# One of the seven block products of a hidden layer done by seven products of its own blocks

## The chip, the cores and the metric

One core of a Trainium2 chip. The metric is the device time of one launch in microseconds (us), the median of three runs. All numbers are fp32 unless said otherwise.

## What is computed

4096 tokens of 512 features pass a modulated linear layer; each of 8 experts then picks the 1024 tokens with its highest softmax score, runs a two-layer network on them and adds the result, times the score, to the tokens' rows. Most of the work is in the two `einsum`s over the experts.

```python
y = clip(einsum('blc,oc->blo', x * styles, weight) * dcoefs + bias, -256, 256)
scores = softmax(y @ Wr)                        # 4096 x 8
G, idx = top_k(scores.T, 1024)                  # for each expert
h = gelu(einsum('ekd,edh->ekh', y[idx], W1) + b1)     # 512 -> 2048
X_e = einsum('ekh,ehd->ekd', h, W2) + b2              # 2048 -> 512
out = x + zeros.at[idx].add(G * X_e)
```

## The kernel before

**The frame.** A first part (about the first 180 us) makes the layer's output y, its scores and the first expert's token list. Then follow 16 passes: `for e in range(E)` over 8 experts and `for p in range(NP)` over two halves of the hidden width (L1205 to L1228). A pass has a hidden stage (W1 times tokens, 1024 hidden values of 1024 tokens, into the tile H) and an output stage (H times W2, added into the rows of `out` by an indirect DMA on GpSimd, L1156).

**Seven products for eight.** Both stages cut their matrices in two by two blocks and use the scheme with seven block products and fifteen sums. The functions are named after the products: p1 and p2 make the first block of the result; p6, p7, p5, p3, p4 the others. p1, p6, p5 and p3 all add into one PSUM bank, "a": p1 starts it, ScalarE copies the bank out (`snap`, L1059 for hidden, L1123 for output), p6 adds to it, and so on, so that each later product of "a" must wait for the copy of the state before. p7 and p4 share a bank "c" in the same way, p2 has a bank "b". The sums of one operand are made by `left_sums` (L929 to L932: s3, s1, s2, s4), those of the weights by `weight_sum_steps` (L190 to L193: t1, t2, t4, t3), all on VectorE.

**A hidden unit** (`hidden_unit`, L1031) is one of four row blocks of 128 hidden values; each of its seven products is two matmuls (contraction 256) of 512 tokens. p2 is the product of block "12" of the tokens with block (1,0) of W1; its bank is added to p1's copy (L1072) and passed through Gelu (L1073). p5's copy minus bank "c" (L1087) and bank "c" plus p6's copy (L1096) give two other blocks, p3's bank the last; each goes through Gelu into H.

**An output unit** (`out_unit`, L1102) is one of four blocks of 128 tokens (and of 128 more in the other half); its products are four matmuls each (contraction 512) of 256 columns. Its operand's sums are made from H into tiles hs_o. p1 needs the block of H that p1 and p2 of the hidden units make, p2 that of p3, and p6 needs s2, to which every block but one of H contributes; the last to come is that of p4.

**What sets the order.** `in_turns` (L999) calls the steps: p1 of a unit, then the p3 that the unit before still owes, p2, then the p4 owed, then p6, p7, p5. Work "between" (the sums of weights, the next expert's indices and gathers `fetch`, its token preparation `prepare`, and `route_others` in the first pass, which finds the other experts' thresholds by counting) is tied behind a unit by `issue_after`. Otherwise a scheduler chooses the order on each engine: `product` (L1025) issues its matmuls without `in_order`, so that matmuls of one stage can be placed among those of another. `in_order` (L77) ties each instruction behind the one before on TensorE.

**Feeding.** Weights come by DMA on the SP queue: `load_w1` of the next pass is called after the hidden stage, `load_w2` after the output stage. The next expert's tokens are gathered row by row on GpSimd (L913) into four buffers with the tag "row", written to DRAM from there by the SP queue (L917), read back in another layout (L919) and transposed on VectorE (L952). The token lists come from `indices` (L834): VectorE compares places with a row of numbers (L849, one instruction of 4096 elements), TensorE sums (L855), VectorE rounds (L860).

Of the kernel before, what the change touches and what calls it, by code (L numbers as in the profile page):

```python
# [20 lines left out]
P = 128  # L21
# [4 lines left out]
def tile_modulated_expert_choice_ffn(  # L26
# [73 lines left out]


    NL = P // E
    pk = const.tile([P, P], I32, name="pk")
    nc.gpsimd.iota(pk, pattern=[[0, P]], base=0, channel_multiplier=1)
    pm = const.tile([P, P], I32, name="pm")
    nc.gpsimd.iota(pm, pattern=[[1, P]], base=0, channel_multiplier=0)
    ek = const.tile([P, P], I32, name="ek")
    nc.vector.tensor_scalar(ek, pk, E - 1, None, op0=ALU.bitwise_and)
    em = const.tile([P, P], I32, name="em")
    nc.vector.tensor_scalar(em, pm, E - 1, None, op0=ALU.bitwise_and)  # L110
    same = const.tile([P, P], BF16, name="same")
    nc.vector.tensor_tensor(same, ek, em, ALU.is_equal)
    ahead = const.tile([P, P], BF16, name="ahead")
    nc.vector.tensor_tensor(ahead, pk, pm, ALU.is_lt)
    nc.vector.tensor_mul(ahead, ahead, same)


    iota_lo = const.tile([P, P], BF16, name="iota_lo")
# [44 lines left out]
    HP = HC // NP  # L163
    U = HP // 2
    QD = D // 2
    w1_blocks, w2_blocks = {}, {}

    def weight_blocks(kind, where, name):
# [26 lines left out]
    def weight_sums(kind, blk, name):  # L195
        for _ in weight_sum_steps(kind, blk, name):
            pass

    def load_w1(e, ps):
        where = {}  # L200
# [535 lines left out]

    def route_others():

        ST = rt.tile([P, 2, P], F32, tag="ST", name="ST")
# [12 lines left out]

        mark = rt.tile([P, 2, P], F32, tag="run", name="mark")
# [17 lines left out]

        def ranks(mask, name):

            run = rt.tile([P, 2, P], F32, tag="run", name=f"run_{name}")
# [12 lines left out]
            nc.vector.tensor_copy(off, ps)  # L789
            return run, off  # L790


        sel = rt.tile([P, 2, P], F32, name="sel")
# [3 lines left out]
        eq = rt.tile([P, 2, P], F32, name="eq")  # L797
# [19 lines left out]
        for h in range(2):  # L817
            nc.tensor.transpose(ps[:, h, :], pos[:, h, :], ident)

        pos_i = rt.tile([P, NT, E], I32, tag="ST", name="pos_i")  # L820
        nc.vector.tensor_scalar(pos_i.rearrange("p t e -> p (t e)"),
                                ps.rearrange("p h m -> p (h m)"), -1.0, None, op0=ALU.add)
        part = rt.tile([P, NT, E], I32, tag="part", name="part")
# [3 lines left out]
        part2 = rt.tile([P, NT, E], I32, tag="part", name="part2")  # L827
        nc.vector.tensor_scalar(part2, pos_i, 7, None, op0=ALU.logical_shift_right)
        hi = rt.tile([P, NT, E], BF16, name="hi")
        nc.vector.tensor_copy(hi, part2)  # L830
        for e in range(1, E):
            places[e] = lo[:, :, e], hi[:, :, e]

    def indices(e):  # L834

        lo, hi = places[e]
        oh = gp.tile([P, 2 * GH * YW], BF16, tag="xg", name=f"oh_{e}")[:, 0 : NT * P].rearrange(
            "p (t m) -> p t m", m=P)
        hot = rt2.tile([P, NT, KG], BF16, tag="hot", name=f"hot_{e}")
        nc.vector.tensor_tensor(  # L840
            hot, hi.unsqueeze(2).to_broadcast([P, NT, KG]),
            iota_hi[:, 0:KG].unsqueeze(1).to_broadcast([P, NT, KG]), ALU.is_equal,
        )
        val = rt2.tile([P, NT, 2, KG], BF16, tag="val", name=f"val_{e}")
        nc.vector.tensor_scalar_mul(val[:, :, 0, :], hot, iota_p[:, 0:1])
        nc.vector.tensor_tensor(
            val[:, :, 1, :], hot, iota_t.unsqueeze(2).to_broadcast([P, NT, KG]), ALU.mult
        )
        nc.vector.tensor_tensor(  # L849
            oh, lo.unsqueeze(2).to_broadcast([P, NT, P]),  # L850
            iota_lo.unsqueeze(1).to_broadcast([P, NT, P]), ALU.is_equal,
        )
        ps = ps_small.tile([P, 2, KG], F32, tag="small", name=f"ps_idx{e}")
        for t in range(NT):
            nc.tensor.matmul(ps.rearrange("p a k -> p (a k)"), oh[:, t, :],  # L855
                             val[:, t, :, :].rearrange("p a k -> p (a k)"),
                             start=(t == 0), stop=(t == NT - 1))
# [46 lines left out]
    def gather(e, i):  # L904
# [31 lines left out]
    def token_tiles(e):  # L936
# [6 lines left out]
        tokens[e] = {**s, "11": xT[0, 0], "12": xT[0, 1], "22": xT[1, 1]}, gain, ngain  # L943
        return xT, s, gain, ngain

    def prepare(e):

        xT, s, gain, ngain = token_tiles(e)
# [5 lines left out]
                    xg[:, :, 2 * k * TB : 2 * (k + 1) * TB].rearrange("p t (j a) -> p t j a", a=TB))  # L954
        nc.vector.tensor_scalar_mul(ngain, gain, -1.0)
        left_sums(xT[0, 0], xT[0, 1], xT[1, 0], xT[1, 1], s)

    def first_tokens(started):

# [39 lines left out]
    def in_turns(units, between):  # L999

# [4 lines left out]
        for n in range(len(units)):  # L1005
# [15 lines left out]
            held = unit[5:]  # L1021
        for f in held:
            f()

    def product(ps, lefts, rights, start):  # L1025
        n = len(lefts)
        for k in range(n):
            nc.tensor.matmul(ps, lefts[k], rights[k], start=(start and k == 0), stop=(k == n - 1),  # L1028
                             skip_group_check=True)

    def hidden_unit(e, p, u, H, early=False):  # L1031

# [7 lines left out]
        def mm(ps, left, right, start):  # L1040
            s = tokens[e][0]
            product(ps, [blk[right][:, k, u * P : (u + 1) * P] for k in range(2)],
                    [s[left][:, k, :] for k in range(2)], start)

        def begin(cols):
            s = tokens[e][0]

# [7 lines left out]
                                     skip_group_check=True))  # L1055

        def snap(n):
            t = sp.tile([P, HALF], F32, tag=f"snap{n}", name=f"snap{n}_{name}")
            nc.scalar.copy(t, st["a"])  # L1059
            return t  # L1060

# [3 lines left out]
                mm(st["a"], "11", (0, 0), True)  # L1065
            st["s1"] = snap(1)

        def p2():
            if not early:
                st["b"] = bank("b", name, 1)  # L1070
                mm(st["b"], "12", (1, 0), True)
            added = nc.vector.tensor_add(st["b"], st["b"], st["s1"])  # L1072
            nc.scalar.activation(out[0, 0], st["b"], AF.Gelu, bias=bias[0])  # L1073
            return added

        def p6():
# [20 lines left out]
            nc.scalar.activation(out[1, 0], st["c"], AF.Gelu, bias=bias[0])  # L1097

        unit = [p1, p2, p6, p7, p5, p3, p4]
        return (begin, unit) if early else unit  # L1100

    def out_unit(e, p, v, H, b2_sb):  # L1102

# [101 lines left out]
    for e in range(E):  # L1205
        b2_sb = fx.tile([P, D], F32, tag="b2", name=f"b2_{e}")
        nc.sync.dma_start(b2_sb, b2[e, :].partition_broadcast(P))
        for p in range(NP):
# [60 lines left out]
```

## Time and profile before

| what | value |
|---|---|
| runs | 1745.69, 1746.89, 1747.21 us; median 1746.89 |
| profiled execution | 1745.7 us; its span, first to last instruction, 1743.9 us; granted clock 0.996 |
| VectorE, ScalarE, GpSimd busy | 830.8, 480.2, 293.5 us |
| fp32 matmul of a hidden unit, 512 columns | 593 ns recorded each, two records a matmul |
| fp32 matmul of an output unit, 256 columns | 380 ns recorded each, two records a matmul |
| weight load of 128 columns | 190 ns |
| copy of a bank by ScalarE, 512 and 256 columns | 582 and 474 ns |
| add of a bank on VectorE, 512 and 256 columns | 699 and about 480 ns |
| sum of 512, 1024 elements in SBUF on VectorE | 687, about 1217 ns |
| comparison with the row of numbers, L849 | 4418 ns, seven times |
| gather of 128 rows, issue to landing | 4.3 us |

How to read the profile: matmuls are pipelined, so a recorded duration is longer than the distance from one to the next; the chain that ended last counts each only for the time in which nothing later had started, which is the price in a stream. "PEld" is TensorE's weight load, which overlaps with matmuls. In a line of the timeline, the bracket at the end holds how long the engine stood idle before the instruction and what it waited for. Names are those of the program, with "_h" for hidden and "_o" for output.

### The profile page before, as it was taken

How to read it: one execution, taken by the hardware profiler on the slowest of the kernel's cores; microseconds unless marked ns; L12 is line 12 of the kernel's file. 1: busy time of each engine (PE TensorE's matmuls, PEld its weight loads, DVE VectorE, ACT ScalarE, POOL GpSimd, SP SyncE). 2: the span in 40 equal slices, each digit the busy share in tenths (PEclk: the TensorE clock that was granted, in tenths of full speed). 3: DMA queues.
4: the chain of work that ended last, by engine and by line, in shares of the span. 5: the costliest groups of instructions: out<-in, count | busy, mean ns of one | idle time of the engine just before them, and what ended most of it. 6: DMA issues, size and time to landing. Idle time of an engine off the chain costs nothing.

```text
span 1743.9 us, 17415 instructions
## 1 busy us (share of the span) xinstructions
PE 1718.0 (99%) x6646; PEld 1136.2 (65%) x6646; DVE 830.8 (48%) x1467; ACT 480.2 (28%) x845; POOL 293.5 (17%) x238
## 2 busy tenths in 40 slices
PE   9998999999999999999999999999999999999997
PEld 5775475665748485766758485766758484756656
DVE  5885884524535254624535254614444254614341
ACT  3543312223131322222231313222231313222231
POOL 0112013020212013110312012110302012110202
PEclk9999999999999999999999999999999999999999
DMA  9625527441574237442574237432564137332403
GB/s 207 171 50 197 192 55 179 106 85 49 97 201 73 48 61 183 90 85 55 100 191 85 49 63 176 90 79 55 112 179 90 46 64 186 75 79 61 85 0 49
DMA packets 143252, 178.59 MB, mean 102 GB/s; under 512 B 16825, under 2 KB 92857, under 8 KB 143041
## 3 DMA queue, kind: packets, MB, share of 16 engines
q1 hardware_dynamic: 118240, 115.19, 24.4%
q0 software_dynamic: 24912, 62.27, 21.0%
q8 instruction: 52, 0.85, 0.2%
q14 instruction: 32, 0.25, 0.0%
q10 hardware_dynamic: 16, 0.02, 0.0%
HBM read 120.46 MB, written 65.37 MB: 107 GB/s over the span
## 4 chain that ended last, share of the span: by engine, by line
PE 93%; DVE 4%; ACT 1%; issue 1%; DMA 1%; POOL 0%; POOLq 0%; DVEq 0%; ACTq 0%
PE ps_a_o L1028 25%; PE ps_a_h L1028 23%; PE ps_c_o L1028 12%; PE ps_c_h L1028 12%; PE ps_b_o L1028 6%; PE ps_b_h L1028 6%; PE ps_ya L81 2%; PE ps_yc L81 1%; DVE oh L849 1%; PE ps_y L81 1%; ACT xmT L500 1%; DVE mark L760 1%; PE ps_yt L727 1%; PE ps_a_h_a L1028 0%; PE ps_yb L81 0%
## 5 line engine op out<-in xcount | busy, mean ns | idle before, releaser
L1156 POOL DMA_INDIRECT out<-o_o,idx x128 | 213.2, 1666 | 1246.7 <-DVE o_o L1153 497.0
L1028 PE MATMUL ps_a_o<-w_t,hs_o 128*128 128x256 f32 x1024 | 243.3, 380 | 1.2
L1028 PE MATMUL ps_a_h<-xs,w_t 128*128 128x512 f32 x496 | 233.4, 592 | 0.0
L1028 PEld LDWEIGHTS ps_a_o<-w_t,hs_o 128*128 128x128 f32 x1024 | 192.3, 190 | 33.7 <-issue 7.2
L1028 PEld LDWEIGHTS ps_a_h<-xs,w_t 128*128 128x128 f32 x496 | 94.1, 190 | 119.1 <-issue 118.5
L1059 ACT COPY snap_h<-ps_a_h 128x512 f32<-128x512 f32 x186 | 108.2, 582 | 230.0 <-PE ps_a_h L1028 227.0
L1123 ACT ACTIVATE snap_o<-ps_a_o,gain 128x256 f32<-128x256 f32 x128 | 60.6, 474 | 346.7 <-PE ps_a_o L1028 346.7
L1087 DVE TENSOR_TENSOR snap_h<-snap_h,ps_c_h 128x512 f32<-128x512 f32 x64 | 43.9, 687 | 217.5 <-ACT snap_h L1059 217.5
L1072 DVE TENSOR_TENSOR ps_b_h<-ps_b_h,snap_h 128x512 f32<-128x512 f32 x62 | 43.4, 699 | 202.6 <-PE ps_b_h L1028 202.6
L1028 PE MATMUL ps_c_o<-w,hs_o 128*128 128x256 f32 x512 | 124.2, 380 | 0.0
L1028 PE MATMUL ps_a_o<-w,H 128*128 128x256 f32 x512 | 124.0, 379 | 0.0
L1028 PE MATMUL ps_a_o<-w,hs_o 128*128 128x256 f32 x512 | 121.6, 380 | 0.0
L1028 PE MATMUL ps_b_o<-w,H 128*128 128x256 f32 x512 | 121.1, 379 | 0.0
L1028 PE MATMUL ps_a_h<-xT,w 128*128 128x512 f32 x248 | 120.7, 594 | 0.0
L1028 PE MATMUL ps_c_h<-xs,w 128*128 128x512 f32 x256 | 120.5, 593 | 0.0
L1028 PE MATMUL ps_c_h<-xT,w_t 128*128 128x512 f32 x256 | 120.5, 593 | 0.0
L1028 PE MATMUL ps_c_o<-w_t,H 128*128 128x256 f32 x504 | 119.1, 379 | 0.0
L1028 PE MATMUL ps_a_h<-xs,w 128*128 128x512 f32 x248 | 118.2, 599 | 0.0
L1028 PE MATMUL ps_b_h<-xT,w 128*128 128x512 f32 x248 | 116.8, 593 | 0.0
L1028 PEld LDWEIGHTS ps_a_o<-w,H 128*128 128x128 f32 x512 | 97.1, 190 | 27.0 <-issue 15.5
L1028 PEld LDWEIGHTS ps_a_o<-w,hs_o 128*128 128x128 f32 x512 | 95.9, 190 | 21.8 <-ACT snap_o L1123 9.2
L1028 PEld LDWEIGHTS ps_c_o<-w,hs_o 128*128 128x128 f32 x512 | 97.0, 190 | 13.9 <-issue 0.6
(277 smaller groups left out, 1983.8 us busy)
## 6 DMA issues: line engine op xcount, KB each, us to landing
w<-in_w SPq DMA_DIRECT2D x120, 512.0 KB, 4.1
rows<-row SPq DMA_DIRECT2D x56, 260.0 KB, 3.9
xg<-rows SPq DMA_DIRECT2D x56, 256.0 KB, 6.4
x<-in_x SPq DMA_DIRECT2D x28, 256.0 KB, 8.4
y_dram<-ytok SPq DMA_DIRECT2D x5, 1024.0 KB, 4.3
w<-in_w SPq DMA_DIRECT2D x32, 128.0 KB, 3.5
y_dram<-ytok POOLq DMA_DIRECT2D x12, 256.0 KB, 5.0
b<-in_b SPq DMA_DIRECT2D x8, 256.0 KB, 4.2
```

The source lines that it names most:

```text
L81: behind[engine] = make()
L500: nc.scalar.mul(t, t, styles[1][:, j, b : b + 1])
L727: nc.tensor.transpose(ps[:, o * P : (o + 1) * P], yT[:, o, t * P : (t + 1) * P], ident)
L760: nc.vector.tensor_scalar(mark, ST, cand[:, c + 1 : c + 2].bitcast(F32), None, op0=ALU.is_ge, op1=ALU.add, accum_out=cnt[:, c : c + 1])
L849: nc.vector.tensor_tensor(oh, lo.unsqueeze(2).to_broadcast([P, NT, P]), iota_lo.unsqueeze(1).to_broadcast([P, NT, P]), ALU.is_equal,)
L1028: nc.tensor.matmul(ps, lefts[k], rights[k], start=(start and k == 0), stop=(k == n - 1), skip_group_check=True)
L1059: nc.scalar.copy(t, st["a"])
L1072: added = nc.vector.tensor_add(st["b"], st["b"], st["s1"])
L1087: nc.vector.tensor_add(st["u4"], st["u4"], st["c"])
L1123: nc.scalar.mul(t, st["a"], scale)
L1156: nc.gpsimd.indirect_dma_start(out=last_rows[g] if e == E - 1 else out_rows, out_offset=bass.IndirectOffsetOnAxis(ap=idx[:, e, g : g + 1], ...
```

## The change

In every hidden stage but the first, p2 is no longer two matmuls a unit. Its operands (W1's block (1,0): 256 by 512; the tokens' block "12": 256 by 512) are cut in two by two once more, and the same seven-product scheme runs on blocks of 128 by 256 and 128 by 256, for two row blocks r of 128 (and of 128 more). That makes 14 products of one matmul each, 256 columns wide, in place of 8 matmuls of 512 columns. Each has a bank of its own from the pools "t" (a and c) or "b"; results are collected in a tile q, and p2 of a unit becomes an addition of a part of q to p1's copy, in SBUF.

`hidden_stage` writes the order by hand: the 14 products stand one by one behind products of the units, which now run in the order 0, 2, 1, 3. `product` issues every matmul through `in_order`, in both stages. The p3 and p4 that the last output unit owes are held over into the next hidden stage and run behind its first p1 and p6; `load_w2` is called behind that p4.

The sums for the second level are added: four of 256 elements per weight block (in `weight_sums`) and four per token block (`second_sums`). To find room in SBUF, several buffers are shared or dropped: "row" has three buffers, not four; s1 of an output unit is written over its part of H (the block (1,0)) instead of into a tile of its own; the tiles of `route_others` lie in the row buffers; the second sums lie in the buffer of a token block no longer needed. `indices` does its comparison in four instructions of 1024 elements.

```diff
@@ weight_sums
+        if kind == "w1":
+            b = {(k, j): blk[1, 0][:, k, j * Q : (j + 1) * Q] for k in range(2) for j in range(2)}
+            t = wpool.tile([P, 3, Q], F32, tag="w1_l2", name=f"w1_l2_{name}")
+            t1, t2, t4 = [t[:, n, :] for n in range(3)]
+            nc.vector.tensor_add(t1, b[0, 0], b[0, 1])
+            nc.vector.tensor_add(t2, t1, b[1, 1])
+            nc.vector.tensor_add(t4, t2, b[1, 0])
+            nc.vector.tensor_add(b[0, 1], b[0, 1], b[1, 1])
+            blk["l2"] = {**b, "t1": t1, "t2": t2, "t3": b[0, 1], "t4": t4}
@@ indices
-        nc.vector.tensor_tensor(
-            oh, lo.unsqueeze(2).to_broadcast([P, NT, P]),
-            iota_lo.unsqueeze(1).to_broadcast([P, NT, P]), ALU.is_equal,
-        )
+        for n in range(4):
+            here = slice(n * NT // 4, (n + 1) * NT // 4)
+            nc.vector.tensor_tensor(
+                oh[:, here, :], lo[:, here].unsqueeze(2).to_broadcast([P, NT // 4, P]),
+                iota_lo.unsqueeze(1).to_broadcast([P, NT // 4, P]), ALU.is_equal,
+            )
@@ gather
-            to = gp.tile([P, YW], F32, tag="row", name=f"row_{e}_{g}", bufs=4)
+            to = gp.tile([P, YW], F32, tag="row", name=f"row_{e}_{g}", bufs=3)
@@ new
+    def second_sums(e):
+        s = tokens[e][0]
+        a = {(i, k): s["12"][:, k, i * Q : (i + 1) * Q] for i in range(2) for k in range(2)}
+        t = fx.tile([P, 4, Q], F32, tag="xT10", name=f"x2_{e}")
+        s2 = {f"s{n + 1}": t[:, n, :] for n in range(4)}
+        left_sums(a[0, 0], a[0, 1], a[1, 0], a[1, 1], s2)
+        tokens[e][0]["l2"] = {**s2, "11": a[0, 0], "12": a[0, 1], "22": a[1, 1]}
@@ product
-            nc.tensor.matmul(ps, lefts[k], rights[k], start=(start and k == 0), stop=(k == n - 1),
-                             skip_group_check=True)
+            in_order(partial(nc.tensor.matmul, ps, lefts[k], rights[k], start=(start and k == 0),
+                             stop=(k == n - 1), skip_group_check=True))
@@ new
+    def second_level(e, p, r):
...
+        def mm(tag, left, right, start):
+            if start:
+                st[tag] = (bank("b", f"q{name}", 1) if tag == "b" else
+                           ps_t.tile([P, HALF], F32, tag="t", name=f"ps_q{tag}_{name}"))[:, 0:Q]
+            product(st[tag], [blk[right][:, r * P : (r + 1) * P]], [s[left]], start)
...
+        def p5():
+            mm("a", "s1", "t1", False)
+            st["u4"] = snap(4, -1.0)
+            nc.vector.tensor_sub(out[1, 1], st["u4"], st["c"])
...
+    def hidden_stage(e, p, H, between, held, then):
+        unit = {u: hidden_unit(e, p, u, H) for u in range(U)}
+        steps, results = zip(*[second_level(e, p, r) for r in range(2)])
...
+        plan = [
+            (0, [partial(second, 0)], [partial(second, 0)], [partial(second, 0)], [partial(second, 0)],
+             [partial(second, 0)], []),
+            (2, [], [partial(second, 0)], [partial(second, 0), partial(finish, 0), partial(finish, 2)],
+             [partial(second, 1)], [partial(second, 1)], [partial(second, 1)]),
+            (1, [partial(second, 1)], [partial(second, 1)], [], [partial(second, 1)],
+             [partial(second, 1), partial(finish, 1)], []),
+            (3, [partial(finish, 3)], [], [], [], [], []),
+        ]
+        for n, (u, *fill) in enumerate(plan):
+            p1, _, p6, p7, p5, p3, p4 = unit[u]
+            for f, behind_it in zip((p1, held[0], p6, held[1], p7, p5), fill):
+                f()
+                if n == 0 and f is held[1]:
+                    then()
+                for step in behind_it:
+                    mark = step() or mark
...
+            held = [p3, p4]
+        for f in held:
+            f()
@@ hidden_unit
-        def p2():
-            if not early:
-                st["b"] = bank("b", name, 1)
-                mm(st["b"], "12", (1, 0), True)
-            added = nc.vector.tensor_add(st["b"], st["b"], st["s1"])
-            nc.scalar.activation(out[0, 0], st["b"], AF.Gelu, bias=bias[0])
+        def p2(other=None):
+            to = st["s1"] if other is not None else st["b"]
+            added = nc.vector.tensor_add(to, st["b"] if other is None else other, st["s1"])
+            nc.scalar.activation(out[0, 0], to, AF.Gelu, bias=bias[0])
             return added
@@ out_unit
-             for n in ("s1", "s2", "s3", "s4")}
+             for n in ("s2", "s3", "s4")}
+        s["s1"] = a[1, 0]
         left_sums(a[0, 0], a[0, 1], a[1, 0], a[1, 1], s)
@@ main loop
-            units = [partial(hidden_unit, e, p, u, H) for u in range(U)]
             if e == p == 0:
+                units = [partial(hidden_unit, e, p, u, H) for u in range(U)]
                 units[0:2] = [lambda unit=unit: unit for _, unit in early]
-            in_turns(units, work)
+                in_turns(units, work)
+            else:
+                hidden_stage(e, p, H, work, held, partial(load_w2, e, p))
...
-            in_turns([partial(out_unit, e, p, v, H, b2_sb) for v in range(GH)], work)
-            if nxt[0] < E:
-                load_w2(*nxt)
+            if e == p == 0:
+                work[0] = [partial(second_sums, 0)]
+            held = in_turns([partial(out_unit, e, p, v, H, b2_sb) for v in range(GH)], work,
+                            keep=nxt[0] < E)
```

More of the change, by code (lines that the diff above doesn't have):

```diff
@@ L102, in tile_modulated_expert_choice_ffn @@
     NL = P // E
[L103 to L110, printed above, removed]
     same = const.tile([P, P], BF16, name="same")
-    nc.vector.tensor_tensor(same, ek, em, ALU.is_equal)
     ahead = const.tile([P, P], BF16, name="ahead")
-    nc.vector.tensor_tensor(ahead, pk, pm, ALU.is_lt)
-    nc.vector.tensor_mul(ahead, ahead, same)
+    with tc.tile_pool(name="init", bufs=1) as init:
+        pk = init.tile([P, P], I32, name="pk")
+        nc.gpsimd.iota(pk, pattern=[[0, P]], base=0, channel_multiplier=1)
+        pm = init.tile([P, P], I32, name="pm")
+        nc.gpsimd.iota(pm, pattern=[[1, P]], base=0, channel_multiplier=0)
+        ek = init.tile([P, P], I32, name="ek")
+        nc.vector.tensor_scalar(ek, pk, E - 1, None, op0=ALU.bitwise_and)
+        em = init.tile([P, P], I32, name="em")
+        nc.vector.tensor_scalar(em, pm, E - 1, None, op0=ALU.bitwise_and)
+        nc.vector.tensor_tensor(same, ek, em, ALU.is_equal)
+        nc.vector.tensor_tensor(ahead, pk, pm, ALU.is_lt)
+        nc.vector.tensor_mul(ahead, ahead, same)
     iota_lo = const.tile([P, P], BF16, name="iota_lo")
@@ L165, in tile_modulated_expert_choice_ffn @@
     QD = D // 2
+    Q = HALF // 2
     w1_blocks, w2_blocks = {}, {}
@@ L737, in route_others @@
     def route_others():
-        ST = rt.tile([P, 2, P], F32, tag="ST", name="ST")
+        spare = [gp.tile([P, YW], F32, tag="row", name=f"spare{n}", bufs=3) for n in range(3)]
+        ST, run_, sel, eq, part_ = [
+            spare[n // 2][:, n % 2 * 2 * P : (n % 2 + 1) * 2 * P].rearrange("p (h t) -> p h t", t=P)
+            for n in range(5)]
         ps = ps_t.tile([P, 2, P], F32, tag="t", name="ps_ST")
@@ L751, in total @@
             return ps
-        mark = rt.tile([P, 2, P], F32, tag="run", name="mark")
+        mark = run_
         cand = two_bits[:, 0, :]
@@ L774, in ranks @@
         def ranks(mask, name):
-            run = rt.tile([P, 2, P], F32, tag="run", name=f"run_{name}")
+            run = run_
             nc.vector.tensor_tensor_scan(run.rearrange("p h t -> p (h t)"),
@@ L790, in ranks @@
             return run, off
-        sel = rt.tile([P, 2, P], F32, name="sel")
         cnt = rt2.tile([P, 1], BF16, tag="cnt", name="cnt_gt")
@@ L796, in route_others @@
         tot = total(cnt, "gt")
-        eq = rt.tile([P, 2, P], F32, name="eq")
         nc.vector.tensor_scalar(eq, ST, thr, None, op0=ALU.is_equal)
@@ L818, in route_others @@
             nc.tensor.transpose(ps[:, h, :], pos[:, h, :], ident)
-        pos_i = rt.tile([P, NT, E], I32, tag="ST", name="pos_i")
+        pos_i, part = [t.bitcast(I32).rearrange("p h t -> p (h t)").rearrange("p (t e) -> p t e", e=E)
+                       for t in (ST, part_)]
         nc.vector.tensor_scalar(pos_i.rearrange("p t e -> p (t e)"),
                                 ps.rearrange("p h m -> p (h m)"), -1.0, None, op0=ALU.add)
-        part = rt.tile([P, NT, E], I32, tag="part", name="part")
         nc.vector.tensor_scalar(part, pos_i, P - 1, None, op0=ALU.bitwise_and)
@@ L826, in route_others @@
         nc.vector.tensor_copy(lo, part)
-        part2 = rt.tile([P, NT, E], I32, tag="part", name="part2")
-        nc.vector.tensor_scalar(part2, pos_i, 7, None, op0=ALU.logical_shift_right)
+        nc.vector.tensor_scalar(part, pos_i, 7, None, op0=ALU.logical_shift_right)
         hi = rt.tile([P, NT, E], BF16, name="hi")
-        nc.vector.tensor_copy(hi, part2)
+        nc.vector.tensor_copy(hi, part)
         for e in range(1, E):
@@ L956, in prepare @@
         left_sums(xT[0, 0], xT[0, 1], xT[1, 0], xT[1, 1], s)
+        second_sums(e)
     def first_tokens(started):
@@ L997, in bank, with in_turns @@
         return ps_mm.tile([P, HALF], F32, tag=tag, name=f"ps_{tag}_{name}", bufs=bufs)
-    def in_turns(units, between):
+    def in_turns(units, between, keep=False):
         held = []
@@ L1021, in in_turns @@
             held = unit[5:]
+        if keep:
+            return held
         for f in held:
@@ L1027, in product, with snap, p1, p2 @@
         for k in range(n):
-            nc.tensor.matmul(ps, lefts[k], rights[k], start=(start and k == 0), stop=(k == n - 1),
-                             skip_group_check=True)
+            in_order(partial(nc.tensor.matmul, ps, lefts[k], rights[k], start=(start and k == 0),
+                             stop=(k == n - 1), skip_group_check=True))
+    def second_level(e, p, r):
+        s, blk = tokens[e][0]["l2"], w1_blocks[e, p]["l2"]
+        name = f"{e}_{p}_{r}"
+        q = sp.tile([P, 2, HALF], F32, tag="q", name=f"q_{name}", bufs=1)
+        out = {(i, j): q[:, j, i * Q : (i + 1) * Q] for i in range(2) for j in range(2)}
+        st = {}
+        def mm(tag, left, right, start):
[3 more added lines that the diff above has]
+            product(st[tag], [blk[right][:, r * P : (r + 1) * P]], [s[left]], start)
+        def snap(n, scale=1.0):
+            t = sp.tile([P, Q], F32, tag=f"q{n}", name=f"q{n}_{name}", bufs=1)
+            nc.scalar.mul(t, st["a"], scale)
+            return t
+        def p1():
+            mm("a", "11", (0, 0), True)
+            st["s1"] = snap(1)
+        def p2():
+            mm("b", "12", (1, 0), True)
+            return nc.vector.tensor_add(out[0, 0], st["b"], st["s1"])
+        def p6():
+            mm("a", "s2", "t2", False)
+            st["u2"] = snap(2)
+        def p7():
+            mm("c", "s3", "t3", True)
+        def p5():
+            mm("a", "s1", "t1", False)
+            st["u4"] = snap(4, -1.0)
+            nc.vector.tensor_sub(out[1, 1], st["u4"], st["c"])
+        def p3():
+            mm("a", "s4", (1, 1), False)
+            nc.scalar.mul(out[0, 1], st["a"], -1.0)
+        def p4():
+            mm("c", "22", "t4", False)
+            nc.vector.tensor_add(out[1, 0], st["c"], st["u2"])
+        return [p1, p2, p6, p7, p5, p3, p4], q
@@ new lines, in hidden_stage, with finish, second @@
+    def hidden_stage(e, p, H, between, held, then):
+        unit = {u: hidden_unit(e, p, u, H) for u in range(U)}
+        steps, results = zip(*[second_level(e, p, r) for r in range(2)])
+        g = [iter(x) for x in steps]
+        def finish(u):
+            return unit[u][1](results[u % 2][:, u // 2, :])
+        def second(r, n=1):
+            for _ in range(n):
+                done = next(g[r])()
+            return done
+        mark = None
+        plan = [
[15 more added lines that the diff above has]
+                    mark = step() or mark
+            for work in between.get(n, ()):
+                with tc.issue_after(mark.ins):
+                    work()
+            held = [p3, p4]
+        for f in held:
+            f()
@@ L1043, in mm, with second_product @@
                     [s[left][:, k, :] for k in range(2)], start)
+        def second_product():
+            st["b"] = bank("b", name, 1)
+            mm(st["b"], "12", (1, 0), True)
+            return p2()
         def begin(cols):
@@ L1057, in snap @@
         def snap(n):
-            t = sp.tile([P, HALF], F32, tag=f"snap{n}", name=f"snap{n}_{name}")
+            t = sp.tile([P, HALF], F32, tag=f"snap{n}", name=f"snap{n}_{name}",
+                        bufs=3 if n == 1 else 2)
             nc.scalar.copy(t, st["a"])
@@ L1099, in hidden_unit @@
         unit = [p1, p2, p6, p7, p5, p3, p4]
-        return (begin, unit) if early else unit
+        if early:
+            return begin, unit
+        if e == p == 0:
+            unit[1] = second_product
+        return unit
     def out_unit(e, p, v, H, b2_sb):
@@ L1225, in tile_modulated_expert_choice_ffn @@
                 work[0] = [partial(prepare, e + 1)]
-            in_turns([partial(out_unit, e, p, v, H, b2_sb) for v in range(GH)], work)
-            if nxt[0] < E:
-                load_w2(*nxt)
+            if e == p == 0:
+                work[0] = [partial(second_sums, 0)]
+            held = in_turns([partial(out_unit, e, p, v, H, b2_sb) for v in range(GH)], work,
+                            keep=nxt[0] < E)
 def kernel(**inputs):
```

## The prediction

> **What bounds the kernel now.** I read the page first, for the busy shares and the chain that ended last; columns are busy time, share and instruction count, then shares of the span.
>
> ```profile
> PE 1718.0 (99%) x6646; PEld 1136.2 (65%) x6646; DVE 830.8 (48%) x1467; ACT 480.2 (28%) x845; POOL 293.5 (17%) x238
> PE 93%; DVE 4%; ACT 1%; issue 1%; DMA 1%; POOL 0%; POOLq 0%; DVEq 0%; ACTq 0%
> ```
>
> The chain is TensorE for 93% of the span, so time is won or lost only in TensorE's own queue: in the matmuls that stand there, and in the moments when it waits between two. The second view is busy time by stretches, cut at the same point of four successive passes (one pass is a hidden stage and an output stage; columns: length, PE busy, PEld busy, DVE, ACT, POOL, clock, DMA share, GB/s).
>
> ```profile
> 421.46:519.47 98.01, 97.88 (x369) 64.25 (x369) 44.39 (x62) 25.42 (x45) 21.61 (x16) 1.00 0.58 132
> 519.47:616.38 96.91, 96.83 (x338) 63.55 (x337) 41.85 (x57) 25.32 (x45) 12.96 (x8) 1.00 0.31 66
> ```
>
> A pass takes 96.9 us, or 98.0 where the next expert's indices are computed (32 small matmuls, 0.96 us, and their surroundings). VectorE works 42 to 44 us of it, ScalarE 25: both have room. The third view is the chain across the seam between a hidden and an output stage (start, length, work; _h is hidden, _o output).
>
> ```profile
> 414.45 1.72 PE ps_a_h L1028 x4
> 416.16 0.86 PE ps_a_o L1028 x4
> 417.03 1.85 PE ps_a_h L1028 x4
> 418.88 1.72 PE ps_c_h L1028 x4
> 420.60 0.86 PE ps_a_o L1028 x4
> 421.46 1.73 PE ps_b_o L1028 x8
> 423.19 0.86 PE ps_c_o L1028 x4
> 424.05 0.08 issue
> 424.13 1.96 PE ps_a_o L1028 x8
> 426.09 0.86 PE ps_c_o L1028 x4
> ```
>
> Two things are to be seen. The price of a matmul instruction: 1.72/4 = 0.429 us at 512 columns, 1.73/8 = 0.216 at 256 (each fp32 matmul is two instructions). And the scheduler has filled the seam: half of the output's p1 (0.86) lies between the last unit's p5 and p3, and half of its p7 (0.86) ahead of its p6. The check: 4 x 7 x 4 x 0.429 = 48.1 us and 4 x 7 x 8 x 0.216 = 48.4 make 96.4 of the 96.9, so 0.5 us is lost per pass, 0.44 of it here: 1.85 for 1.72, 0.08, and 1.96 for 1.73. The fourth view is the timeline of the same seam, the other engines' instructions that these waits hang on.
>
> ```profile
> 416.26 0.59 ACT L1059 COPY snap_h<-ps_a_h 128x512 f32<-128x512 f32 x1 [2.85 <-PE ps_a_h L1028]
> 416.89 0.30 PEld L1028 LDWEIGHTS ps_a_h<-xs,w 128*128 128x128 f32 x2 [0.27 <-ACT snap_h L1059]
> 420.63 0.70 DVE L1096 TENSOR_TENSOR ps_c_h<-ps_c_h,snap_h 128x512 f32<-128x512 f32 x1 [3.07 <-PE ps_c_h L1028]
> 421.37 0.69 ACT L1097 ACTIVATE H<-ps_c_h,b_sb 128x512 f32<-128x512 f32 x1 [1.76 <-DVE ps_c_h L1096]
> 422.09 0.69 DVE L929 TENSOR_TENSOR hs_o<-H 128x512 f32<-128x512 f32 x1 [0.75 <-ACT H L1097]
> 422.69 0.69 DVE L930 TENSOR_TENSOR hs_o<-H 128x512 f32<-128x512 f32 x1
> 423.30 0.69 DVE L931 SCALAR_TENSOR_TENSOR hs_o<-hs_o,H 128x512 f32<-128x512 f32 x1
> 423.90 0.68 DVE L929 TENSOR_TENSOR hs_o<-H 128x512 f32<-128x512 f32 x1
> ```
>
> p3 may not load its weights before the copy of p5's bank is done (416.89); the output's p6 waits for p4, its add, its Gelu and the sums s3, s1, s2 (423.99).
>
> **What the Trainium skill says.** "TensorE: Matmul & The Clock Gate", Back-to-back issue gap: in a stream of weight loads and matmuls the spacing is set by both. That would threaten narrow products; here the load takes 190 ns under a spacing of 216, so 256 columns still stream, as the output stage shows. "VectorE: DVE Perf Modes", The DRAIN you can't avoid: the next operation waits until the pipe is empty, and a semaphore between two costs nothing extra. The trace agrees: dependent and independent sums both follow at 0.60 to 0.61. So a sum put ahead of another delays it by 0.60.
>
> **The change, part by part.** *The product replaced.* In 15 of 16 hidden stages (not the first) p2 was 4 units x 4 instructions x 0.429 = 6.87 us of TensorE. In its place: 2 row blocks x 7 products x 2 instructions of 256 columns = 28 x 0.216 = 6.05. Saved: 0.82 us a stage, on the path. Instructions at this width and size fill the output stage, so the price is shown.
>
> *Its waits.* Each bank that is copied and then added to needs about 0.7 us (0.10 + 0.59) of other matmuls between. In the written order the shortest cover is one 512-wide product (1.72) everywhere, or 2.6 in the first unit (0.43 + 1.73 + 0.43), but for one place: the last unit's p5 and p3, which follow each other.
>
> *The seam.* All products now go out in written order, and the changed program's instruction order confirms that nothing of the output stage stands between p5, p3 and p4 or ahead of p6. p3's release is the same copy, so p3 still ends 2.72 us after p5 (416.16 to 418.88) and p4 after 4.44; but the 0.86 of p1 that was done inside this time is now done later. Then come p1 and p2, 3.46 us, and p6, which waits for s2. VectorE's order here is no longer s3, s1, s2: s1 is written over part of H and s3 of the second output unit stands ahead of it in all 15 stages, so s2 is 0.60 later. Before, p6 ended 426.09 - 420.60 = 5.49 after p4; now 6.09. From p5 to the end of p6: 4.44 + 6.09 = 10.53, against 9.93 before, which held 0.86 of p7 as well, so 9.07 for the same products. Loss 1.46 us a seam. If the restart of p3 without cover is as quick as the weight load's record (0.14 quicker), it is 1.46 still, as long as s2 decides after p4; p4 and s2 would come 0.14 sooner, so 1.32 is the lower end. Upper end 1.6.
>
> *The other seam.* The output's last p3 and p4 now run among the first hidden products; these were filled before (one p3 of 1.76 for 1.73). Zero.
>
> *Beside the path.* ScalarE gets 8 pieces of 0.47 us a pass, 3.8 on 25. VectorE gets 6 adds of 0.48; the four final adds replace L1072's at the same length; the second sums are 4 of 0.42 (an estimate: 0.69 at 512 and 1.22 at 1024 give 1.03 ns an element) per token block and per weight block, with over 40 us idle in a pass. They are hidden by TensorE; uncovered they would cost 3.4 a pass.
>
> *Indices.* They now come after the first unit's p5, 12.5 us into the stage. VectorE starts after the first row block's add (4.8): 0.75 for an output row, 0.33, four pieces of 1.16 (4.42/4 and 0.06), 0.55 for the values, 0.48 and 0.75 for two output adds queued between: 12.25. In time, and the last piece gates only 8 of 32 matmuls. Cost 0; between -0.2 and +1 in 7 stages.
>
> *Buffers and queues.* With three row buffers the fourth gather waits for the first store: 5.4 us later (483.44 to about 488.9), twice; the SP queue, whose loads stand behind these stores, has the second half some 10 us later. Its first user is the transpose at 527.97, 44 us after. Zero; if that cover failed, up to 5 us in 7 passes. The w2 loads wait for the output's p3, 4 us into the stage, and are needed 36 us in.
>
> *The first pass* is bound by VectorE's counting (L760) up to 232.75. There TensorE had done 21 of the output's short matmuls; in the new order 18: 3 x 0.43 = 1.3 later. Then one small matmul waits behind 1.73 us of products for 2.3 us of VectorE work (three second sums of 0.42 stand in it), and one behind 0.43 for about 1.7: 0.6 and 1.2. Sum 3.1; between 0 and 4.
>
> **Sum.** 15 x (1.46 - 0.82) = 9.6, and 3.1: +12.7 us. The profiled execution took 1745.7 (span 1743.9), the median 1746.9 lies 1.2 above: 1758.4 and 1759.6. I take 1759.
>
> **Rivals.** *The seam is even:* s2 is not held up (s3 of the second unit falls into a gap), the loss is 0.86 against 0.82: 15 x 0.04 + 3.1, about 1750. The view by order speaks against it: that sum stands there and nothing else is ready. *Faster:* the Gelu-and-sums path is over when p2 ends. Then p5 to p6 is 1.00 + 8.63 = 9.63, the loss 0.56, and each seam wins 0.26: with a covered first pass 1747 - 4 = 1743, at best 1741. It decides from s2's end 3.09 us after p4; the trace has 3.39 and the new order 3.99. *More waits:* the indices or gathers come late, 1 us or more in 7 passes: 1766 and above. For it: VectorE's margin of 0.3 us; against it: TensorE's other work.
>
> **How the numbers follow.** As worked 0.62 (1754 to 1763); even 0.14 (1747 to 1752); faster 0.10 (1739 to 1744); more waits 0.14 (1763 to 1773). The range 1747 to 1768 leaves out the fast case and half of the last. A measurement of this kernel tells 0.2%, 3.5 us, from no change: faster 0.09, same 0.14, slower 0.77.
>
> **What would show it.** After: passes of about 97.5 and 98.7 us; in the chain at the seam p5, a gap near 0.9, p3, p4, p1, p2, a gap of 0.6 to 0.7, p6; hidden stages without another gap. Wrong if the passes are below 96.9, if p6 follows p2 at once, or if gaps lie among the second-level products.

## The result and the profile after

The changed kernel takes 1755.21 us in the median of five runs (1754.26 to 1756.23), the kernel before 1745.94 on the same chip (five runs, 1744.67 to 1747.21): the ratio is 1.0053, 95% interval 1.0038 to 1.0067. It is slower, by half a per cent. The profiled spans are 1753.8 and 1743.9 us at the same granted clock, 0.996.

The page of the changed kernel, busy times and the chain that ended last:

```profile
PE 1705.4 (97%) x6826; PEld 1173.2 (67%) x6826; DVE 896.6 (51%) x1670; ACT 518.5 (30%) x965; POOL 313.3 (18%) x238
PE 90%; DVE 5%; ACT 2%; DMA 1%; issue 1%; SPq 0%; POOL 0%; POOLq 0%; ACTq 0%; DVEq 0%
```

TensorE is busy for 12.6 us less than before (1718.0), about the 15 x 0.82 = 12.3 that the seven products should save (e3 and e9 below test it); yet the span is 9.9 longer. The chain tells where that went: VectorE and ScalarE, 5% of it before, are now 7%. Two lines of the page's groups put a place to it (the numbers behind the bar: busy, mean ns of one, idle time of the engine just before the group and what ended most of it):

```profile
L81 PE MATMUL ps_a_o<-w_t,hs_o 128*128 128x256 f32 x512 | 122.3, 382 | 10.8 <-DVE hs_o L945 10.2
L81 PE MATMUL ps_a_h<-xs,w 128*128 128x512 f32 x248 | 118.3, 599 | 11.7 <-ACT snap_h L1185 11.7
```

Output p6 waits for s2 (L945), 10.2 us in 15 waits, 0.68 each, and hidden p3 for the copy of the bank (L1185), 11.7 us in 16 waits, 0.73 each: the first hidden stage, which has no second level, is tied too. After each wait the product itself takes about 0.25 longer (1.97 and 1.98 for 1.73), so a seam, the place where a hidden stage meets its output stage, loses about 1.90. Before, it lost 0.44 in all. The chain over one such seam, to be laid beside the one of before (start, length, work):

```profile
514.60 1.73 PE ps_a_h L81 x4
516.33 0.02 issue
...
516.41 0.59 ACT snap_h L1185
517.01 0.04 issue
517.05 1.98 PE ps_a_h L81 x4
519.03 1.73 PE ps_c_h L81 x4
...
520.79 0.71 DVE ps_c_h L1221
521.50 0.02 issue
521.52 0.70 ACT H L1222
522.22 0.02 issue
522.24 1.29 DVE hs_o L943 x2
523.54 0.60 DVE H L944
524.14 0.61 DVE hs_o L945
524.75 0.14 issue
524.88 1.97 PE ps_a_o L81 x8
526.85 1.73 PE ps_c_o L81 x8
```

p5 ends at 516.33, p3 starts only at 517.05, and p6 only at 524.88, behind add, Gelu and four sums: two s3 (L943 x2), s1 and s2. p1 and p2 of the output stage, 3.46 us, run beside that chain and don't fill it. Before, half of p1 stood between p5 and p3.

The measure for all that follows is the length of a pass, from the last output unit's p2 to the next pass's (the piece "PE ps_b_o" of the chain). It repeats to about 0.03 us within a run after the first two passes, and does not depend on how long the first part of the program took. All passes come in two kinds, without and with the next expert's indices.

| kernel | pass | pass with indices | ratio to before (95% interval) |
|---|---|---|---|
| before | 96.90 | 98.02 | 1 |
| changed | 97.51 | 98.40 | 1.0053 (1.0038 to 1.0067) |
| e1 sums of unit 0 first | 97.03 | 97.93 | 1.0013 (1.0006 to 1.0019) |
| e2 seam filled | 96.61 | 97.51 | 0.9978 (0.9969 to 0.9987) |
| e3 no second level | 98.33 | 99.23 | 1.0124 (1.0108 to 1.0139) |
| e4 before, in order | 98.62 | 99.74 | 1.0156 (1.0142 to 1.0169) |
| e5 filled, p7 halved, sums first | 96.16 | 97.07 | 0.9945 (0.9931 to 0.9958) |
| e6 filled, p7 halved | 96.64 | 97.54 | 0.9980 (0.9973 to 0.9987) |
| e7 output untied | 95.78 | 96.68 | 0.9903 (0.9888 to 0.9918) |
| e8 one comparison | 97.51 | 98.40 | 1.0058 (1.0044 to 1.0072) |
| e9 untied, no second level | 96.60 | 97.50 | 0.9968 (0.9956 to 0.9980) |
| e10 changed, again | 97.51 | 98.40 | 1.0049 (1.0035 to 1.0063) |
| e11 as e7, again | 95.78 | 96.67 | 0.9892 (0.9877 to 0.9907) |

Ratios are to the kernel before on the same chip; its medians there were 1746.15 (e1 to e4), 1751.46 (e5 to e8) and 1746.30 (e9 to e11). On the second chip the part ahead of the first hidden stage took 3 to 9 us longer, so spans aren't compared across chips; the passes agree to 0.01.

### The profile page after: what moved, and what is told of

The parts are those of the page before. It is cut to its first block, busy times and chain, and to the rows that moved or that the text cites. A ratio compares the mean times of both kernels' runs of the same rounds, so it can differ in the third digit from the quotient of the medians.

```text
span 1753.8 us, 18024 instructions
## 1 busy us (share of the span) xinstructions
PE 1705.4 (97%) x6826; PEld 1173.2 (67%) x6826; DVE 896.6 (51%) x1670; ACT 518.5 (30%) x965; POOL 313.3 (18%) x238
## 4 chain that ended last, share of the span: by engine, by line
PE 90%; DVE 5%; ACT 2%; DMA 1%; issue 1%; SPq 0%; POOL 0%; POOLq 0%; ACTq 0%; DVEq 0%
PE ps_a_h L81 24%; PE ps_a_o L81 23%; PE ps_c_o L81 12%; PE ps_c_h L81 12%; PE ps_b_o L81 5%; PE ps_qa L81 3%; PE ps_ya L81 2%; PE ps_qc L81 1%; DVE hs_o L943 1%; PE ps_yc L81 1%; PE ps_a_h_a L81 1%; PE ps_b_q L81 1%; PE ps_y L81 1%; ACT xmT L512 1%; DVE ps_c_h L1221 1%
## 5 line engine op out<-in xcount | busy, mean ns | idle before, releaser
L1286 POOL DMA_INDIRECT out<-o_o,idx x128 | 233.3, 1822 | 1209.1 <-DVE o_o L1283 529.1
L1185 ACT COPY snap_h<-ps_a_h 128x512 f32<-128x512 f32 x186 | 108.3, 582 | 198.6 <-PE ps_a_h L81 194.3
L81 PE MATMUL ps_a_o<-w_t,hs_o 128*128 128x256 f32 x512 | 122.3, 382 | 10.8 <-DVE hs_o L945 10.2
L81 PE MATMUL ps_a_h<-xs,w 128*128 128x512 f32 x248 | 118.3, 599 | 11.7 <-ACT snap_h L1185 11.7
L81 PE MATMUL ps_a_o<-w_t,H 128*128 128x256 f32 x512 | 121.2, 379 | 0.0
L81 PE MATMUL ps_a_h<-xT,w 128*128 128x512 f32 x248 | 117.1, 594 | 0.0
L81 PEld LDWEIGHTS ps_a_o<-w_t,hs_o 128*128 128x128 f32 x512 | 95.9, 190 | 29.5 <-issue 17.2
L81 PEld LDWEIGHTS ps_a_o<-w_t,H 128*128 128x128 f32 x512 | 97.2, 190 | 13.4 <-issue 0.2
L81 PEld LDWEIGHTS ps_b_o<-w,H 128*128 128x128 f32 x512 | 97.3, 190 | 13.2
```

What stands on the lines that cost most here:

```text
L81: behind[engine] = make()
L1286: nc.gpsimd.indirect_dma_start(out=last_rows[g] if e == E - 1 else out_rows, out_offset=bass.IndirectOffsetOnAxis(ap=idx[:, e, g : g + 1], ...
```

## The experiments

**e1, the sums in their old order.** In the changed kernel, s3 of the second output unit is tied behind s2 of the first; nothing else.

```diff
+        with ExitStack() as later:
+            if v == 1:
+                later.enter_context(tc.issue_after(first_made[0].ins))
+            first_made[0] = left_sums(a[0, 0], a[0, 1], a[1, 0], a[1, 1], s)
```

> The changed kernel with one order restored on VectorE: s3 of the second output unit is tied behind s2 of the first, so s3, s1, s2 follow one another again. Theory (the seam: a bare restart of p3 and a late s2, against 0.82 us saved by the second level): s2 comes 0.60 us sooner in 15 seams, 15 x 0.60 = 9.0, so 1755.2 - 9.0 = 1746, within 0.2% of the kernel before; the gap ahead of p6 shrinks from 0.68 to about 0.08. Rival (the second level or the shared buffers cost the time, the seam is not decisive): no change, 1755.

Measured: 1748.76 us, span 1746.2, 7.6 shorter than the changed kernel's; passes shorter by 0.48, times 15 is 7.2. So the order of the sums is on the path, but for 0.48 and not 0.60; p6 still waits 0.2 (3.1 us in 15 waits), where 0.08 was expected. VectorE's timeline over the seam shows the rest (start, length, operation):

```profile
520.73 0.69 DVE L943 TENSOR_TENSOR hs_o<-H 128x512 f32<-128x512 f32 x1 [0.75 <-ACT H L1224]
521.46 0.69 DVE L944 TENSOR_TENSOR H<-H 128x512 f32<-128x512 f32 x1
522.06 0.68 DVE L945 SCALAR_TENSOR_TENSOR hs_o<-hs_o,H 128x512 f32<-128x512 f32 x1
```

s1 (L944) starts 0.73 after s3, not 0.60: it is now written over the block of H that s3 has just read, and in the trace it waits for VectorE's own semaphore. With another sum in between, as in the changed kernel, that wait costs nothing (0.60). So taking the foreign s3 away gives back 0.48 of the 0.60 by which s2 was late, and the shared buffer keeps 0.12. This split is read off the timelines; no run gave s1 its own tile back.

**e2, the seam filled.** Half of p1 is put between the last hidden p5 and p3, half behind p4, and all of p7 ahead of p6; p3 and p4 of the last unit are handed over to the output stage for that, and `load_w1` is called behind that p4.

```diff
@@ hidden_stage
-        for f in held:
-            f()
+        return held
@@ in_turns, first output unit
+            if n == 0 and handed:
+                unit, begin, sums = unit
+                begin()
+                handed(sums)
...
+                first[2:4] = first[3], first[2]
```

> The changed kernel with the seam filled by hand: half of the output's p1 between the last unit's p5 and p3, the other half after p4, and p7 ahead of p6. VectorE's order is left as it is. Theory: p3 finds 0.86 us of work in its 1.00, and p6 has 0.86 + 1.73 + 1.73 = 4.32 of work behind p4 where s2 and the restart need 4.36. Lost at a seam about 0.2 in place of 1.90: 15 x 1.7 = 25 us, so about 1730, faster than both kernels by 0.9% or more. Rival (the time is lost elsewhere): at most a few us, 1750 to 1755.

Measured: 1741.95 us, span 1739.7. Its span is 14.1 below the changed kernel's and 4.2 below that of the one before, but the time is some 12 us above the 1730 expected. The seam of this run in the chain, around p3 and from p2 on, and a line of the waits (total, times, longest):

```profile
514.08 0.86 PE ps_a_o L81 x4
514.95 1.85 PE ps_a_h L81 x4
...
519.38 1.73 PE ps_b_o L81 x8
521.10 1.73 PE ps_c_o L81 x8
522.83 1.80 PE ps_a_o L81 x8
524.63 0.02 issue
524.65 0.48 ACT snap_o L1260
525.13 0.04 issue
525.18 1.99 PE ps_a_o L81 x8
```

```profile
PE ps_a_o L81 <- ACT snap_o L1260: 8.5, 15, 0.6
```

p6 now follows p7 at once, and p3 (1.85 for 1.72) has its cover: the two old waits are gone. But p5 must wait for the copy of p6's bank, and p7 was what used to stand between the two. The wait has moved one product on: 0.55 idle and 1.99 - 1.73 = 0.26 of restart, 0.81 a seam, 15 x 0.81 = 12.2. My edit had made it, and the expectation had left it out.

**e3, the second level taken out.** The changed kernel with p2 as matmuls of 512 columns again, all else kept, the order by hand, the shared buffers and the sums of the second level too. One of these sums is written over a quarter of W1's block (1,0), which p2 then reads, so p2 here works on a block in which that quarter holds a sum.

```diff
-        steps, results = zip(*[second_level(e, p, r) for r in range(2)])
...
+        for n, u in enumerate((0, 2, 1, 3)):
+            fill = [[], [unit[u][1]], [], [], [], []]
```

> The changed kernel with the second level's products taken out and p2 back as two matmuls of 512 columns a unit, behind the p3 that is owed; written order, shared buffers and the second level's sums stay. Theory: TensorE gets 15 x 0.82 = 12.3 us more, the seam as in the changed kernel: 1767. Rival (the second level brings nothing or costs): 1755 or less.

Measured: 1768.68 us, span 1768.8; passes 98.33, so the second level saves 98.33 - 97.51 = 0.82 a pass, to the hundredth what 6.87 - 6.05 gives.

**e4, the kernel before with its matmuls tied.** Only `product` is changed.

```diff
-            nc.tensor.matmul(ps, lefts[k], rights[k], start=(start and k == 0), stop=(k == n - 1),
-                             skip_group_check=True)
+            in_order(partial(nc.tensor.matmul, ps, lefts[k], rights[k], start=(start and k == 0),
+                             stop=(k == n - 1), skip_group_check=True))
```

> The kernel before with one line of the change: the matmuls of each product issued in written order, nothing else. Theory: both seams lose their filling. Hidden to output: 0.86 a pass (VectorE's order is the old one). Output to hidden: p3 waits 0.10 + 0.47 for its copy and 0.3 to restart, 0.85 a pass. 15 x 1.7 and about 1.5 in the first pass, 27 us: 1773. Rival (the order of the matmuls matters little, the chain is fixed by the sums): 1746 to 1750.

Measured: 1773.8 us, span 1772.9: the tie alone costs 98.62 - 96.90 = 1.72 a pass. Its chain shows two bare seams, each about half of that. At hidden to output p5 to the end of p6 takes 9.91, against 10.52 in the changed kernel; the 0.61 between is s2's delay. At output to hidden it has what neither of the two kernels has:

```profile
469.82 1.74 PE ps_a_o L81 x8
...
471.65 0.48 ACT snap_o L1123
472.13 0.04 issue
472.17 1.99 PE ps_a_o L81 x8
```

The changed kernel fills that seam by hand, with the p3 and p4 that it holds over.

**e5 and e6, p7 in halves around p6.** Both start from e2; e5 has the sums in e1's order as well.

```diff
+        def p7_around_p6():
+            st["c"] = bank("c", name, 2)[:, 0:QD]
+            for n, ks in enumerate((range(2), range(2, U))):
+                product(st["c"], [s["s3"][:, k, :] for k in ks],
+                        [blk["t3"][:, k, :] for k in ks], n == 0)
+                if n == 0:
+                    p6()
```

> The seam of the run before with half of p1 between p5 and p3, now with p7 cut in halves around p6 and with the sums of the first output unit ahead of those of the second (s2 then ends at about 521.9 on that run's clock, when half of p7 ends at 521.96). Theory: the 12 us by which the filled seam fell short of its expectation are the bare wait of p5 for the copy of p6's bank (0.55 idle and 0.27 of restart, 15 times), because all of p7 had been put ahead of p6. Half of p7 (0.86) behind p6 covers that copy, half ahead of p6 covers the sums: span 1739.7 - 15 x 0.82 = 1727.4, pass near 95.8. Rival: the shortfall has another place (weights called later, the other seam): span 1738 to 1740, and the gap before p5 gone all the same.

> As the run beside it, p7 in halves around p6, but with VectorE's order left as the scheduler makes it (the second output unit's s3 ahead of the first unit's s1 and s2). Theory: the order of the sums costs 0.6 on the path as soon as only half of p7 stands ahead of p6: p6 waits for s2 (released at 522.6 on the filled seam's clock, half of p7 done at 521.96): 0.6 to 0.8 a seam comes back, span 1727.4 + 15 x 0.7 = 1738, about that of the filled seam with p7 whole. Rival: the order of the sums doesn't matter once the seam is filled: 1728.

Measured: passes 96.16 (e5) and 96.64 (e6), against 96.61 in e2; 1740.95 and 1747.54 us on a chip where the kernel before took 1751.46. The wait of p5 is gone in both, as expected. What is left in its place, first e5's line, then e6's:

```profile
PE ps_a_o L81 <- DVE hs_o L945: 3.1, 15, 0.2
```

```profile
PE ps_a_o L81 <- DVE hs_o L945: 10.2, 15, 0.7
```

e6 gave its gain back to s2, as the theory had it. e5 came out 0.36 above the 95.8 expected: I had taken s2 to be ready as half of p7 ends, but s1's 0.12 (e1) makes it 0.2 late, and any wait at all then costs a restart (p6 1.97 for 1.73).

**e7, the output stage untied.** The changed kernel in which only the output stage's matmuls are given back to the scheduler.

```diff
-    def product(ps, lefts, rights, start):
+    def product(ps, lefts, rights, start, tied=True):
...
-            in_order(partial(nc.tensor.matmul, ps, lefts[k], rights[k], start=(start and k == 0),
+            (in_order if tied else lambda f: f())(partial(nc.tensor.matmul, ps, lefts[k], rights[k], start=(start and k == 0),
...
@@ out_unit, mm
-                    [blk[right][:, k, :] for k in range(U)], start)
+                    [blk[right][:, k, :] for k in range(U)], start, tied=False)
```

> The changed kernel with one part undone: the output stage's matmuls are no longer tied one behind the other, those of the hidden stage and its second level still are. The scheduler puts half of p1 between p5 and p3, p7 ahead of p6, and half of the next unit's p1 between p6 and p5. Theory (the tie on the output stage, not the second level, is what makes the change slower): the seam's 1.46 and more comes back; from the filled seam's run 1739.7 - 15 x 0.82 = 1727.4, and 1 less in the first pass: span 1726, faster than the kernel before by 1%. Rival: the second level's own instructions disturb the stage, so that the seam's gain is lost elsewhere: 1744 or above.

Measured: 1734.01 us, ratio 0.9903, passes 95.78 and 96.68, shorter than the changed kernel's by 1.73 and 1.72. Its span, 1729.8, is 3.8 above the 1726 expected, but its first 512-wide product starts 3.1 later than the changed kernel's (181.54 for 178.41). The seam in the chain of its second measurement (e11):

```profile
512.16 0.86 PE ps_a_o L1056 x4
513.03 1.85 PE ps_a_h L81 x4
514.88 1.72 PE ps_c_h L81 x4
516.60 0.86 PE ps_a_o L1056 x4
517.46 1.73 PE ps_b_o L1056 x8
519.18 1.73 PE ps_c_o L1056 x8
520.91 6.96 PE ps_a_o L1056 x32
```

There is no engine but TensorE in it. The scheduler has done what e2 did, and one thing more: half of the next unit's p1 stands between p6 and p5 (the x32 holds p6, p5, p3 and p1 of the next unit), which covers the copy that e2 left bare.

**e8, the comparison in one piece.** Changed kernel, with the 4096 elements in one instruction again.

```diff
-        for n in range(4):
-            here = slice(n * NT // 4, (n + 1) * NT // 4)
-            nc.vector.tensor_tensor(
...
+        nc.vector.tensor_tensor(
+            oh, lo.unsqueeze(2).to_broadcast([P, NT, P]),
+            iota_lo.unsqueeze(1).to_broadcast([P, NT, P]), ALU.is_equal,
+        )
```

> The changed kernel with the comparison of the indices in one instruction of 4096 elements again, at its new place. Passes with indices were 0.23 shorter than the prediction's zero allows (0.79 for the 32 small matmuls, not 0.96). Theory: they run shorter since the four pieces let them start before the comparison is over: undone, 7 x 0.2 = 1.4 longer, span 1755.2, the 32 matmuls at 0.96 and a wait for VectorE ahead of them. Rival: it is the new place behind p5 alone: span 1753.8, the matmuls still 0.79.

Measured: 1762.16 us; passes with indices 98.40, as in the changed kernel, the 32 small matmuls 0.79 as there. The span, 1762.5, is 8.7 above the changed kernel's, but the first 512-wide product starts 8.6 later (187.03 for 178.41). The theory fell: the four pieces bring nothing. Kernels with the old place of the indices have 0.96 or 0.97 for these matmuls and a wait ahead (before, e4), those with the new place 0.79 (changed, e3, e7, e8). The lines, changed and before:

```profile
480.64 0.79 PE ps_idx L869 x32
```

```profile
477.33 0.20 DVE val L845
477.53 0.35 DVE val L846
477.87 0.05 issue
477.92 0.96 PE ps_idx L855 x32
```

At the old place VectorE is late, and the first small matmuls start from a standstill; at the new one the operands are there: in the changed kernel the last piece is done at 480.11. That the place is what counts follows from this comparison of kernels; no run changed the place alone.

**e9 to e11, on one chip.** e9 is e3 and e7 together; the others are repeats.

> The changed kernel with the second level taken out (p2 again as matmuls of 512 columns; it reads a block of W1 of which one quarter has been overwritten by a sum) and with the output stage's matmuls untied. Theory: the second level gives its 0.82 a pass whatever the seam looks like; the 0.30 by which the untied kernel's passes beat before's beyond that (96.90 - 95.78 - 0.82) comes from the seam, where all of p7 stands ahead of p6. So passes of 96.60 and 97.50, ratio to before near 0.997, and 12 us longer than the untied kernel beside it. Rival: the second level's short products fill something at the seams and are worth more than 0.82: passes of 96.9 and 98.0, as before.

> The changed kernel itself, for a comparison on one chip with its untied form: passes 97.51 and 98.40, ratio to before 1.005.

> The changed kernel with the output stage untied, again, on one chip with the changed kernel: passes 95.78 and 96.68, ratio to before 0.990, 27 us (15 x 1.73 and 1.4 in the first pass) shorter than the changed kernel. Rival: part of its gain was another chip's start: 22 us or less.

Measured: 1741.45, 1755.39 and 1728.36 us; passes 96.60, 97.51 and 95.78. The second level saves 0.82 in the untied form as well, and untying takes 27.0 us off (15 x 1.73 = 26, and 1.4 in the first pass). The other 0.30 by which e7's passes beat before's is the same in e9, so it belongs to the order at the seam: before, 0.44 was lost there; in e7 only p3's 0.13 is left.

## Why the prediction was right, and where it was not

The forecast of 1759 us and slower holds in direction, cause and size; 1755.2 is 3.8 below it. Its steps one by one:

- *The product replaced, 0.82 saved a stage:* exactly so (e3 against the changed kernel, e9 against e7).
- *The hidden to output seam, 1.46 lost:* 98.33 - 96.90 = 1.43 (e3 against before). p5 to the end of p6 took 10.52 (526.85 - 516.33) where 10.53 was worked out, and s2 ended 3.99 after p4 (524.75 - 520.76), where the text had 3.99. The two parts of the 1.46 were tried apart: tying the matmuls alone costs 0.84 here (e4: 9.91 against 9.07 for the same products), the sums' order and place 0.61 (changed against e4). Of this, removing the foreign s3 gives back 0.48 (e1). The prediction put all of the 0.60 down to that; 0.12 stays with s1's shared buffer, which the step had named as the reason for the order but not priced. It had read its trace as if a sum that depends on the one directly ahead follows as fast as any other; the lines it shows have no such pair (see the last section).
- *The other seam, 0:* right because the change fills it by hand; e4 shows what it would cost otherwise, about 0.85 (0.61 idle and 1.99 for 1.73).
- *Indices, 0:* missed by -0.23 in 7 passes, -1.6 in all. The prediction asked only whether VectorE would be in time at the new place. It didn't see that before it was late, and so left out a gain; its range ended at -0.2, just short of it. (Its terms for VectorE add up to 12.30, not 12.25; nothing hung on that.)
- *The waits of the second level, buffers and queues, 0:* right; no gap lies among the second level's products. GpSimd's gathers do wait for a row buffer, 4.26 and 4.68 us in one pass, but no wait of TensorE for a gather or a load shows in the passes.
- *The first pass, +3.1:* from the start of its first 512-wide product to its last p2 it went from 82.80 to 85.05, +2.25. Before with tied matmuls (e4) has 85.09 without any second sums: the tie is enough to explain it, and the three second sums that the working had placed on the path were not needed for it. With the output stage untied (e7) it is 83.67. So the tie of the output stage, where the working's three terms (1.3, 0.6, 1.2) lie, costs 1.38, and there is another 0.87 for which it had no term: the total came nearer than its parts, by luck. The kept traces place the 0.87 near the start of the first hidden stage, where the next unit's p1 is long done. Before, half a product of the next unit stood between p5 and p3; in the tied order only one small product (ps_ST) does, and p3 waits for the copy (before, then e11):

```profile
183.55 1.02 PE L1028 MATMUL ps_a_h_a<-xs,w_t 128*128 128x512 f32 x2
184.41 1.88 PE L1028 MATMUL ps_a_h_a<-xs,w 128*128 128x512 f32 x4
```

```profile
184.24 0.38 PE L757 MATMUL ps_ST<-ident,S 128*128 128x128 f32 x2
185.08 1.98 PE L81 MATMUL ps_a_h_a<-xs,w 128*128 128x512 f32 x4 [0.46 <-ACT snap_h L1185]
```

Counted from the first 512-wide product, e11 is 0.83 behind a few products later (194.42 - 179.09 against 192.68 - 178.18). No run filled that place.
- *Profiled execution and median:* the working put the median 1.2 above the profiled execution. Here the profiled execution took 1755.56, 0.35 above the median of 1755.21.

The sum again with these sizes: 8 x 0.61 + 7 x 0.38 = 7.5 for the passes, less 0.3 since the second pass of before took 97.18; 2.25 for the first pass; 0.35 ahead of it and after the last p2: 9.8, and the spans differ by 9.9. What was too high: 1.6 for the indices, 0.85 in the first pass, 15 x 0.03 = 0.5 at the seam, about 1 for the median.

The rivals. *Even seam:* e1 makes its condition true, and gives 1748.8 where it said about 1750; so its mechanism was real and only its premise, a gap for the second s3, was absent, as the order of the instructions had said. *Faster* needed s2 to be early and was not reached; that the path to a faster kernel lay in the matmuls' order at the seam, not in VectorE, it did not see. *More waits* didn't appear.

So the change itself, seven products for one, is worth 0.82 x 15 = 12.3 us, and it was made slower by what came with it, the tie of the output stage's matmuls: with that taken back the kernel runs at 0.989 to 0.990 of before.

## What to carry to other kernels

A written order protects what it was written for and leaves bare the places that a scheduler had been filling; look at both ends of a stage, where the last copy or sum of one meets the first product of the next, before tying a stream. When a cover is moved to fill one wait, ask what it was covering where it stood (e2: the wait ahead of p6 had cost 0.92, and 0.81 came back one product later). And price a repair by the length of a pass, which here tells 0.05 us, rather than by the total, which tells 3.

## What the runs showed of the hardware

- A VectorE sum of 512 fp32 elements that depends on the sum directly ahead of it starts 0.71 to 0.73 us after it; without such a dependence, or with another sum in between, 0.60. In e1 it is s1, which overwrites what s3 reads. The trace of the kernel before has it too, 23 times, where s2 directly follows the s3 that it reads:

```profile
427.30 0.68 DVE L929 TENSOR_TENSOR hs_o<-H 128x512 f32<-128x512 f32 x1
428.02 0.69 DVE L931 SCALAR_TENSOR_TENSOR hs_o<-hs_o,H 128x512 f32<-128x512 f32 x1
```

The prediction read from its lines that dependent and independent sums both follow at 0.60 to 0.61, but there s1 stands between s3 and s2. It cited the Trainium skill, "VectorE: DVE Perf Modes", The DRAIN you can't avoid, for a semaphore that costs nothing extra between two operations. For a wait on the operation directly ahead these traces measure 0.11 to 0.13 more, and the measurement decides.
- A matmul that had to wait costs more than the wait: the first product after it took 1.96 to 1.99 for 1.73, so about 0.25 us, whether the wait was 0.08 (before), 0.2 (e5) or 0.7 (changed). Where the copy is done just in time (p3 behind half of p1) it is 0.13. A wait made shorter gains what it is shortened by (e1: 0.48 a pass), but these 0.25 come back only when it is gone.
